# A two-layer relational graph convolution on one core: preparation at one part per quad, layer 2's weights after it, layer 2's table begun at quad 84

## The chip, the cores and the metric

The kernel runs on one core of a Trainium2 chip. The core has five engines that run side by side and wait for each other through semaphores: PE (matrix multiply), DVE (elementwise), ACT (activation and copies), POOL (here only the issue of gathers) and SP (here only the issue of plain transfers). The metric is the time of one execution on the device, in microseconds (us). Three runs of the kernel before took 4668.13, 4668.17 and 4673.87 us, a median of 4668.17. One more execution was profiled: it took 3997.74 us, and its profile spans 3996.0 us from the first to the last instruction. It is thus 670 us shorter than the runs that were only timed; the two are kept apart below.

## The reference

A graph has N = 12500 nodes with 128 features and E = 200000 edges, each with a source, a destination and one of R = 8 types; edges are sorted by destination. Two layers follow each other, then a residual and a normalization:

```python
W = einsum('rb,bio->rio', comp, basis)          # 8 weights of 128 x 128
msgs = einsum('ni,rio->nro', h, W)[src, et]     # one message per edge
seg = dst * 8 + et
mean = segment_sum(msgs, seg) / maximum(count(seg), 1)
h = h + relu(mean.reshape(N, 8, 128).sum(1) + h @ root + bias)   # twice
out = layernorm(x + h)
```

So each edge's message is divided by the number of edges with the same destination and type. All numbers are float32.

## The kernel before, in words

Edges are cut into 1563 tiles of 128. Four tiles are a quad (391 of them, `q`), eight a group (`g`, two quads), and 128 nodes a block (`k`, 98 of them; about four quads of edges end in one block).

**The gathers.** For every tile, in both layers, POOL issues one indirect transfer that fetches 128 rows of 128 numbers: rows of x in layer 1, rows of the table `y_d` in layer 2 (`gather`, L603). One `gather` call issues a quad. Rows land in a ring of 14 buffers, so the gather of quad q+14 waits until PE has used the rows of quad q; the loop asks for them 12 quads ahead. Three semaphores go round, so a quad's gather also waits for the landing of the one three before.

**Layer 1**, per quad: DVE makes one-hot matrices `dm` scaled by 1/count (`onehot`, L885, for two quads ahead); PE multiplies the gathered rows with them (`means`, L945) and ACT copies the result to `sT`. Per group, PE multiplies the eight types' means with the eight weights (`product`, L966), DVE makes a placement matrix (`place_in`, L977), and PE adds the group's rows to its block (`place`, L999, with the root product at L1001). When a block is full, `finish` adds bias and residual on ACT and DVE (L1015, L1032, L1033) and leaves the block of h in `hT`, in SBUF, where all 98 blocks stay. `table` then makes layer 2's messages of that block for every type: two halves, each one matmul (L1045) and one copy of 128 x 512, the second with the 512 KB store to `y_d` by SP.

**Layer 2** gathers rows of `y_d` with one edge each, sums them with one-hots (L1078), places and finishes as before, and `norms` writes the output. Its first gather waits for the whole of `y_d`. That gives a gap between the layers.

**Preparation.** One-hots and gathers need index tables, in four sets of blocks of 128 tiles. The first set is made before the loop. The others come from a generator, `prep`, inside layer 1's loop. For each set it yields 17 parts from `counts` (one that makes a key from destination and type; 12 that compare the key with itself shifted by four distances each, L726, and add the hits up with eight f16 matmuls, L732 and L733; and four that make `kr`, `w`, `idy` and `slot`, each with a transpose on PE, L689), and two parts more in all for the sources (`sources`, L703, L699). So there are 53 parts. The results of a compare part stand in a ring of two (`eq`).

**Weights.** `weight(l, r)` makes one 128 x 128 weight from eight bases: eight DVE instructions (L618, then L623 seven times). The eight of layer 1 are made before the loop, the eight of layer 2 in its first eight quads.

**Order.** Everything is written out by hand: the Python loop calls the steps in order, `Plan` appends each to the queue of its engine and works out the waits, and each engine runs its own queue strictly in that order. Small jobs hang in the list `todo`: loads and turns of x (`load_x`, `turn_x`), and the halves of the table. One is taken per quad, in three quads of four:

```python
if q % 4 != 3 and todo:
    todo.pop(0)()
if q < R:
    weight(1, q)
if parts is not None:
    if run(parts, 2):
        parts = None
elif later:
    later.pop()()
```

`later` holds the checks of the input's order (`check_edges` and others), one per quad after preparation.

**The arena.** `hT` shares its memory with what is only needed early (edge lists, bases, keys, the compare results). These lie from block `HA` on, so a block of h from there on is written only when what it covers has been read. `HA` is 8.

Of the kernel before, what the change touches and what calls it, by code (L numbers as in the profile page):

```python
# [415 lines left out]
def ordered_path(  # L416
# [30 lines left out]
    R = comp.shape[1]  # L447
# [4 lines left out]
    B = -(-T // P)  # L452
# [12 lines left out]
    S = 8  # L465
    GN = P * S
    NX = -(-N // GN)
    HA = 8
    assert D == P and R * K == P and B == BF + 1 and 1 < TL and LAST < P and BF % 4 == 0 and NQ % 2 == 1 and N % 2 == 0
    main = slice(HALO, HALO + P)  # L470

# [26 lines left out]
    over = {}  # L498
    at = HA * P

# [73 lines left out]
    def vec(emit, reads=(), writes=()):  # L574
        plan.add("DVE", emit, reads, writes)
# [4 lines left out]
    def pe(emit, reads=(), writes=()):  # L580
        plan.add("PE", emit, reads, writes)
# [4 lines left out]
    def load(out_t, in_t, reads=(), writes=(), q="SP"):  # L586
        e = nc.sync if q == "SP" else nc.scalar
        plan.add(q, lambda: e.dma_start(out_t, in_t), reads, writes, lane="hw" if q == "SP" else "aq")

    def copy(out_t, in_t, reads, writes):  # L590
        act(lambda: nc.scalar.activation(out_t, in_t, AF.Copy), reads, writes)  # L591
# [3 lines left out]
    def gather(l, q):  # L595
        if q >= NQ:
            return
        t, cell = rows_r.take()
        rows_g[l, q] = (t, cell)
        ids = idx if l == 0 else idy  # L600

        def emit():
            return [nc.gpsimd.indirect_dma_start(  # L603
                out=t[:, i - q * Q, :], out_offset=None, in_=x if l == 0 else y_d,
                in_offset=bass.IndirectOffsetOnAxis(ap=ids[:, i:i + 1], axis=0))
                for i in range(q * Q, min((q + 1) * Q, T))]

        b = q * Q // P
        reads = ["idx0" if l == 0 and q == 0 else ("idx", b)] if l == 0 else [("idy", b)]
        if l == 1 and q == 0:  # L610
            reads += [("y_d", j) for j in range(NT - 2)] + [("y_d", j, k) for j in (NT - 2, NT - 1) for k in (0, 1)]
        plan.add("POOL", emit, reads, [cell], lane="gq", n=min(Q, T - q * Q))

    def weight(l, r):
        c0 = (l * R + r) * NB

        def emit0():
            return nc.vector.tensor_scalar(w_sb[:, l, r, :], b_sb[:, l, 0, :], comp_sb[:, c0:c0 + 1], None,  # L618
                                           op0=ALU.mult)

        vec(emit0, [("b_sb", l), "comp"], [("w", l, r)])
        for b in range(1, NB):
            vec(lambda b=b: nc.vector.scalar_tensor_tensor(  # L623
                w_sb[:, l, r, :], b_sb[:, l, b, :], comp_sb[:, c0 + b:c0 + b + 1], w_sb[:, l, r, :],
                op0=ALU.mult, op1=ALU.add), [], [("w", l, r)])
# [171 lines left out]
    def check_edges(b):  # L797
        dxc = [("dx", b), ("dx", b, 1), ("dx", b, 2), ("dx", b, 3), ("pad", "dx")]
        t, tc_ = turns.take()
        v1, v2, v3 = (t[:, i, :] for i in range(3))  # L800
        c1, c2, c3 = tc_, tc_ + (1,), tc_ + (2,)
        for emit, r, wr in (
            (lambda: nc.vector.tensor_tensor(v1, dx[:, b, HALO + 1:HALO + P + 1], dx[:, b, main], op=ALU.is_lt),
             dxc, c1),
            (lambda: nc.vector.tensor_tensor(v2, dx[:, b, 2 * HALO:2 * HALO + P], dx[:, b, main], op=ALU.subtract),
             dxc, c2),
            (lambda: nc.vector.tensor_scalar(v3, v2, 250.0, None, op0=ALU.is_gt), [c2], c3),
            (lambda: nc.vector.tensor_tensor(v1, v1, v3, op=ALU.max), [c3], c1),
            (lambda: nc.vector.tensor_scalar(v3, v2, 1.0, None, op0=ALU.is_lt), [c2], c3),
            (lambda: nc.vector.tensor_tensor(v1, v1, v3, op=ALU.max), [c3], c1),  # L810
            (lambda: nc.vector.tensor_reduce(fails[:, b:b + 1], v1, axis=AX.X, op=ALU.max), [c1], ("fails", b)),
        ):
            vec(emit, r, [wr])
# [49 lines left out]
    def rows_of(j):  # L863
        return min(P, N - j * P)
# [11 lines left out]
    def onehot(l, q):  # L876
        if q >= NQ:
            return
        t, cell = dm_r.take()
        dms[l, q] = (t, cell)  # L880
        m, ids = (P, kr) if l == 0 else (2 * K, slot)

        def emit():
            for i in range(q * Q, q * Q + in_quad(q)):
                last = nc.vector.tensor_scalar(t[:, i - q * Q, :m], cols[:, :m], ids[:, i:i + 1],  # L885
                                               w[:, i:i + 1], op0=ALU.is_equal, op1=ALU.mult)
            return last

        b = q * Q // P
        vec(emit, ["cols", ("kr" if l == 0 else "slot", b), ("wt", b)], [cell])  # L890


    def shape_of(n):
        m = min(GN, N - n * GN)
        return (P, S) if m == GN else (m // 2, 2)
# [39 lines left out]
    def two_blocks(g):  # L935
        return (g + 1) // 2 - 1
# [37 lines left out]
    def place_in(g):  # L974
        m = tiles_of(g) * K
        t, c = pl[g] = pl_r.take()
        vec(lambda: nc.vector.tensor_scalar(t[:m], cols[:m], pos[:m, g // (2 * R), g % (2 * R):g % (2 * R) + 1],  # L977
                                            None, op0=ALU.is_equal), ["cols", "pos"], [c])
# [59 lines left out]
    def table(j):  # L1038
        n = rows_of(j)
        yr, yrc = yr_r.take()  # L1040
        split = j >= NT - 2

        def half(k):
            hb, bc = ct_b if split and k == 1 else pt_b
            pe(lambda: nc.tensor.matmul(hb[:n].rearrange("p r d -> p (r d)"), hT[:, j * P:j * P + n],  # L1045
                                        w_sb[:, 1, k * H:(k + 1) * H, :].rearrange("p r d -> p (r d)"),
                                        start=True, stop=True),
               [("h", j)] + [("w", 1, r) for r in range(k * H, (k + 1) * H)], [bc])
            if split and k == 1:
                vec(lambda: nc.vector.tensor_copy(yr[:n, H:, :], hb[:n]), [bc], [yrc + (k,)])  # L1050
            else:
                copy(yr[:n, k * H:(k + 1) * H, :], hb[:n], [bc], [yrc + (k,)])
            if split:
                load(y_d[j * P * R:(j * P + n) * R, :].rearrange("(p r) d -> p r d", r=R)[:, k * H:(k + 1) * H, :],
                     yr[:n, k * H:(k + 1) * H, :], [yrc + (k,)], [("y_d", j, k)])
            elif k == 1:
                load(y_d[j * P * R:(j * P + n) * R, :].rearrange("(p r) d -> p (r d)", r=R),
                     yr[:n].rearrange("p r d -> p (r d)"), [yrc + (0,), yrc + (1,)], [("y_d", j)])

        todo.extend([lambda: half(0), lambda: half(1)])  # L1060

    todo = []


    sum_b = [y_b, ct_b]
# [74 lines left out]
    def run(gen, n):  # L1140
        for _ in range(n):
            if next(gen, gen) is gen:
                return True
        return False
# [23 lines left out]
    def prep():  # L1168
        for i in range(1, len(groups)):
            if i + 1 < len(groups):  # L1170
                sources(*groups[i + 1])
                yield
            yield from counts(i)

    parts = prep()
    later = [lambda b=b: check_edges(b) for b in range(B)]
    later += [check_span, check_place, check_all]
    later.reverse()
    for q in range(NQ - 1):
        g = q * Q // G  # L1180
        gather(0, q + AHEAD)
        onehot(0, q + 2)
        if q == 1:
            where()
        if q % 2 == 0 and g > 0:
            place_in(g - 1)
        means(q)
        if q % 2 == 0:
            if g > 0:
                product(g - 1)  # L1190
        elif g > 0:
            place(0, g - 1)
            k, n = two_blocks(g - 1), two_blocks(g - 1) // S + 1
            if k % S == S // 2 and g % 2 == 1 and n < NX:
                todo.extend([lambda n=n, h=h: turn_x(n, h) for h in range(-(-shape_of(n)[1] // 4))])
                todo.append(lambda n=n: load_x(n + 1))
        if q % 4 != 3 and todo:
            todo.pop(0)()
        if q < R:
            weight(1, q)  # L1200
        if parts is not None:
            if run(parts, 2):
                parts = None
        elif later:
            later.pop()()
    g = NG - 1
    while todo:
        todo.pop(0)()
    place_in(g - 1)
    product(g - 1)  # L1210
    place_in(g)
    means(NQ - 1)
    place(0, g - 1)
    todo.pop(0)()
    product(g)
    todo.pop(0)()
    place(0, g)
    while todo:
        todo.pop(0)()

    for q in range(AHEAD):
        gather(1, q)
# [79 lines left out]
```

## Time and profile before

| | |
|---|---|
| median of three timed runs | 4668.17 us |
| profiled execution | 3997.74 us |
| its span | 3996.0 us |
| POOL busy | 2961.9 us, 74% |
| PE busy | 2093.2 us, 52% |
| DVE busy | 1378.5 us, 34% |
| ACT busy | 565.7 us, 14% |
| mean granted PE clock | 0.675 of full |
| last gather of layer 1, first of layer 2 begin | 2001.8 us, 2019.8 us |

The page gives busy time by engine, the chain of work that ended last, and groups of instructions. In a group's line stand the source line, engine, operation, output and inputs, count, busy time in us, the mean of one in ns, and the engine's idle time just before them with what ended most of it. "issue" is time in which the engine waited for nothing that the profile shows. Lines of a stage view give start and end, the length of the stage, the busy time and count of POOL's gathers in it, the granted PE clock, the busy share of the DMA engines and GB/s. Lines of waits give who waited, for whom, us in total, how often and the longest. Lines of a timeline give start, duration and instruction; its durations overlap where matmuls are pipelined.

### The profile page before, as it was taken

How to read it: one execution, taken by the hardware profiler on the slowest of the kernel's cores; microseconds unless marked ns; L12 is line 12 of the kernel's file. 1: busy time of each engine (PE TensorE's matmuls, PEld its weight loads, DVE VectorE, ACT ScalarE, POOL GpSimd, SP SyncE). 2: the span in 40 equal slices, each digit the busy share in tenths (PEclk: the TensorE clock that was granted, in tenths of full speed). 3: DMA queues.
4: the chain of work that ended last, by engine and by line, in shares of the span. 5: the costliest groups of instructions: out<-in, count | busy, mean ns of one | idle time of the engine just before them, and what ended most of it. 6: DMA issues, size and time to landing. Idle time of an engine off the chain costs nothing.

```text
span 3996.0 us, 33928 instructions
## 1 busy us (share of the span) xinstructions
PE 2093.2 (52%) x11597; PEld 1548.1 (39%) x11597; DVE 1378.5 (34%) x4770; ACT 565.7 (14%) x1238; POOL 2961.9 (74%) x3134
## 2 busy tenths in 40 slices
PE   4787666666666666676633333333333333333333
PEld 3466555555555555555522222222222222222221
DVE  8685333333333333333322332322323323223232
ACT  0123222222222222222200000000000000000000
POOL 7567777777777777777767777777777777777775
PEclk7899888888888878888865555555555555555555
DMA  3123222222222222222222222222222222222221
GB/s 108 52 78 95 79 85 79 85 85 85 79 85 79 85 79 85 85 81 79 79 69 53 64 64 53 63 53 64 63 53 64 63 53 63 53 63 63 53 59 48
DMA packets 128281, 282.59 MB, mean 71 GB/s; under 512 B 53327, under 2 KB 60763, under 8 KB 128099
## 3 DMA queue, kind: packets, MB, share of 16 engines
q0 software_dynamic: 100032, 205.07, 19.7%
q1 hardware_dynamic: 25546, 73.59, 4.9%
q8 instruction: 95, 1.56, 0.2%
q10 hardware_dynamic: 2521, 1.66, 0.2%
q14 instruction: 87, 0.71, 0.1%
HBM read 222.51 MB, written 57.60 MB: 70 GB/s over the span
## 4 chain that ended last, share of the span: by engine, by line
POOL 54%; issue 29%; DMA 7%; PE 4%; DVE 4%; ACT 0%; POOLq 0%; ACTq 0%; DVEq 0%; SPq 0%
POOL rows L603 54%; DMA rows<-in_x_dram,idx 5%; DMA rows<-y_d,idy 2%; PE s L945 1%; PE y L966 1%; DVE w_sb L623 1%; PE ct L732 1%; DVE dm L885 1%; PE ct L733 1%; DVE arena L726 1%; PE pt L1045 0%; PE pt L689 0%; DMA arena<-in_dst_dram 0%; PE po L999 0%; DVE arena L749 0%
## 5 line engine op out<-in xcount | busy, mean ns | idle before, releaser
L603 POOL DMA_INDIRECT rows<-in_x_dram,idx x1563 | 1485.9, 951 | 514.8 <-issue 440.8
L603 POOL DMA_INDIRECT rows<-y_d,idy x1563 | 1474.9, 944 | 493.1 <-issue 464.8
L945 PE MATMUL s<-dm,rows 128*128 128x128 f32 x3126 | 516.0, 317 | 535.6 <-DMA rows<-in_x_dram,idx 533.3
L945 PEld LDWEIGHTS s<-dm,rows 128*128 128x128 f32 x3126 | 454.2, 220 | 720.8 <-DMA rows<-in_x_dram,idx 554.3
L885 DVE TENSOR_SCALAR dm<-cols,kr,w 128x128 f32<-128x128 f32 x1563 | 530.8, 402 | 303.6 <-PE s L945 303.5
L1032 DVE TENSOR_TENSOR v<-po,carry 128x128 f32<-128x128 f32 x196 | 57.0, 291 | 1669.0 <-ACT carry L1015 1666.7
L885 DVE TENSOR_SCALAR dm<-cols,slot,w 128x32 f32<-128x32 f32 x1563 | 374.7, 302 | 501.9 <-PE y L1078 494.2
L1078 PE MATMUL y<-rows,dm 128*32 128x128 f32 x1568 | 210.7, 419 | 642.2 <-DMA rows<-y_d,idy 642.2
L1078 PE MATMUL ct<-rows,dm 128*32 128x128 f32 x1558 | 209.6, 419 | 592.5 <-DMA rows<-y_d,idy 592.5
L966 PE MATMUL y<-w_sb,sT 128*128 128x128 f32 x3136 | 512.0, 333 | 0.0
L966 PEld LDWEIGHTS y<-w_sb,sT 128*128 128x128 f32 x3136 | 500.5, 250 | 1.2 <-issue 1.0
L1078 PEld LDWEIGHTS y<-rows,dm 128*32 128x32 f32 x1568 | 119.2, 158 | 756.0 <-issue 396.7
L1078 PEld LDWEIGHTS ct<-rows,dm 128*32 128x32 f32 x1558 | 119.5, 158 | 666.6 <-issue 423.0
L999 PE MATMUL po<-pl,ys 128*128 128x256 f32 (+1 forms) x784 | 370.4, 567 | 12.2 <-DVE pl L977 9.5
L591 ACT ACTIVATE sT<-s 128x512 f32<-128x512 f32 x391 | 233.4, 597 | 963.8 <-PE s L945 963.5
L591 ACT ACTIVATE ys<-y 128x128 f32<-128x128 f32 (+1 forms) x294 | 81.4, 277 | 1118.5 <-PE y L1078 759.5
L1045 PE MATMUL pt<-w_sb,arena 128*128 128x512 f32 x388 | 208.1, 618 | 2.6 <-DVE arena L1033 2.6
L999 PEld LDWEIGHTS po<-pl,ys 128*128 128x128 f32 (+1 forms) x784 | 163.9, 261 | 89.5 <-issue 79.7
L977 DVE TENSOR_SCALAR pl<-cols,pos 128x256 f32<-128x256 f32 x392 | 186.0, 475 | 0.0
L591 ACT ACTIVATE ys<-ct 128x128 f32<-128x128 f32 x98 | 27.1, 277 | 939.4 <-PE ct L1078 939.4
L591 ACT ACTIVATE y_row<-pt 128x512 f32<-128x512 f32 x194 | 115.8, 597 | 162.1 <-PE pt L1045 162.1
L1015 ACT ACTIVATE carry<-po,bias_t 128x128 f32<-128x128 f32 x196 | 71.6, 365 | 97.3 <-PE po L999 97.3
(114 smaller groups left out, 910.1 us busy)
## 6 DMA issues: line engine op xcount, KB each, us to landing
y_d<-y_row SPq DMA_DIRECT2D x96, 512.0 KB, 2.9
rows<-in_x_dram,idx POOLq DMA_INDIRECT x1563
rows<-y_d,idy POOLq DMA_INDIRECT x1563
x_g<-in_x_dram SPq DMA_DIRECT2D x24, 512.0 KB, 3.7
out_dram<-x_g SPq DMA_DIRECT2D x12, 512.0 KB, 3.0
arena<-in_L_gnn_basis_dram SPq DMA_DIRECT2D x2, 512.0 KB
arena<-in_dst_dram ACTq DMA_DIRECT2D x2, 448.0 KB, 9.1
arena<-in_edge_type_dram SPq DMA_DIRECT2D x2, 448.0 KB, 13.2
```

Of the source, the lines that this page charges most:

```text
L591: act(lambda: nc.scalar.activation(out_t, in_t, AF.Copy), reads, writes)
L603: return [nc.gpsimd.indirect_dma_start(out=t[:, i - q * Q, :], out_offset=None, in_=x if l == 0 else y_d, in_offset=bass.IndirectOffsetOnA ...
L623: vec(lambda b=b: nc.vector.scalar_tensor_tensor(w_sb[:, l, r, :], b_sb[:, l, b, :], comp_sb[:, c0 + b:c0 + b + 1], w_sb[:, l, r, :], op0= ...
L885: last = nc.vector.tensor_scalar(t[:, i - q * Q, :m], cols[:, :m], ids[:, i:i + 1], w[:, i:i + 1], op0=ALU.is_equal, op1=ALU.mult)
L945: last = nc.tensor.matmul(s[:, i, :], t[:, i, :], d[:, i, :P], start=True, stop=True)
L966: last = nc.tensor.matmul(y[:m], t[:, r, :nt, :].rearrange("p t k -> p (t k)"), w_sb[:, 0, r, :], start=(r == 0), stop=(r == R - 1))
L977: vec(lambda: nc.vector.tensor_scalar(t[:m], cols[:m], pos[:m, g // (2 * R), g % (2 * R):g % (2 * R) + 1], None, op0=ALU.is_equal), ["cols ...
L999: ins = nc.tensor.matmul(a, o[:m], t[:m], start=opens, stop=last and not root_in)
L1015: act(lambda: nc.scalar.activation(nt, a[:, P:], AF.Identity, bias=bias_t[:, l:l + 1]), [ac, ("bias_t", l)], [ncell])
L1032: vec(lambda: nc.vector.tensor_add(v[:, :n], a[:, :n], t[:, :n]), [ac, c], [vc])
L1045: pe(lambda: nc.tensor.matmul(hb[:n].rearrange("p r d -> p (r d)"), hT[:, j * P:j * P + n], w_sb[:, 1, k * H:(k + 1) * H, :].rearrange("p ...
L1078: last = nc.tensor.matmul(y[j:j + 2 * K, :], d[:, i, :2 * K], t[:, i, :], start=(i % 2 == 0), stop=(i % 2 == 1 or i == n - 1))
```

## The change

Preparation takes one part per quad in place of two. The eight weights of layer 2 leave the first eight quads and become the first entries of `later`, so they come after preparation and ahead of the checks. The halves of the table go to a list of their own, `tables`, which is opened at quad 84: from there one half is taken in a quad where `todo` is empty and which isn't every fourth. Until then the blocks of h wait in `hT`. Jobs in `todo` may now be taken in every quad. The early data begin at block 24 of the arena in place of block 8. At the end of the loop what is left of both lists is issued, then the last group follows as before.

```diff
-    HA = 8
+    HA = 24
+    TABLE = 84
...
-        todo.extend([lambda: half(0), lambda: half(1)])
-
-    todo = []
+        tables.extend([lambda: half(0), lambda: half(1)])
+
+    todo, tables = [], []
...
-    later = [lambda b=b: check_edges(b) for b in range(B)]
+    later = [lambda r=r: weight(1, r) for r in range(R)] + [lambda b=b: check_edges(b) for b in range(B)]
...
-        if q % 4 != 3 and todo:
+        if todo:
             todo.pop(0)()
-        if q < R:
-            weight(1, q)
+        elif q % 4 != 3 and q >= TABLE and tables:
+            tables.pop(0)()
         if parts is not None:
-            if run(parts, 2):
+            if run(parts, 1):
                 parts = None
         elif later:
             later.pop()()
     g = NG - 1
-    while todo:
-        todo.pop(0)()
+    assert parts is None and not later
+    while todo or tables:
+        (todo or tables).pop(0)()
     place_in(g - 1)
     product(g - 1)
     place_in(g)
     means(NQ - 1)
     place(0, g - 1)
-    todo.pop(0)()
+    tables.pop(0)()
     product(g)
-    todo.pop(0)()
+    tables.pop(0)()
     place(0, g)
-    while todo:
-        todo.pop(0)()
+    while tables:
+        tables.pop(0)()
```

## The prediction

> **What bounds the kernel now.** I read the page first: busy shares, the chain that ended last, the costliest groups.
>
> ```profile
> PE 2093.2 (52%) x11597; PEld 1548.1 (39%) x11597; DVE 1378.5 (34%) x4770; ACT 565.7 (14%) x1238; POOL 2961.9 (74%) x3134
> POOL 54%; issue 29%; DMA 7%; PE 4%; DVE 4%; ACT 0%; POOLq 0%; ACTq 0%; DVEq 0%; SPq 0%
> L603 POOL DMA_INDIRECT rows<-in_x_dram,idx x1563 | 1485.9, 951 | 514.8 <-issue 440.8
> L603 POOL DMA_INDIRECT rows<-y_d,idy x1563 | 1474.9, 944 | 493.1 <-issue 464.8
> ```
>
> POOL's 3126 gathers are nearly the whole span: 0.944 us each and a fixed 0.30 us between two, 1.25 us per tile and 4.99 us per quad of four. 3126 x 1.25 is 3900 of 3996 us. A change can only save what POOL loses beyond that. Where it loses it is in the gathers by stages of 50 us, and in POOL's waits:
>
> ```profile
> 50.00:100.00 50.00, 38.56 (x38) 0.76 0.20 51
> 100.00:150.00 50.00, 26.90 (x27) 0.80 0.16 45
> 150.00:200.00 50.00, 29.22 (x29) 0.93 0.20 59
> 200.00:250.00 50.00, 31.17 (x31) 0.97 0.22 63
> 250.00:300.00 50.00, 37.65 (x40) 1.00 0.31 94
> ```
>
> ```profile
> POOL rows L603 <- issue: 905.6, 2971, 0.5
> POOL rows L603 <- PE s L945: 45.1, 26, 8.0
> POOL rows L603 <- DMA rows<-in_x_dram,idx: 22.6, 74, 0.3
> POOL rows L603 <- DMA y_d<-y_row: 17.1, 1, 17.1
> ```
>
> Steady state is 40 gathers in 50 us; from 100 to 250 us there are 27, 29 and 31. The wait is for PE's `means` (L945), 43.0 us of it before 270 us (the same view for that window), because a gather's buffer is free when `means` of 14 quads earlier is done. The 17.1 us is the gap between the layers.
>
> Why PE is late there, from PE's timeline at full clock:
>
> ```profile
> 211.21 1.05 PE L945 MATMUL s<-dm,rows 128*128 128x128 f32 x8
> 212.10 1.95 PE L966 MATMUL y<-w_sb,sT 128*128 128x128 f32 x16
> 213.89 1.02 PE L1045 MATMUL pt<-w_sb,arena 128*128 128x512 f32 x2
> 214.75 0.38 PE L732 MATMUL ct<-arena,id_h 128*128 128x512 f16 x1
> ...
> 218.22 1.05 PE L945 MATMUL s<-dm,rows 128*128 128x128 f32 x8
> 219.11 0.60 PE L999 MATMUL po<-pl,ys 128*128 128x256 f32 x2
> ```
>
> By start to start: means 0.89 us, product 1.79, half a table 0.86, place 0.43, and two counting parts, 16 f16 matmuls, 3.47 (1.73 a part). From one `means` to the next is 7.0 us where POOL needs 4.99. DVE adds to it: for the first eight quads a weight of layer 2 (one L618, seven L623: 2.9 us) stands in its queue beside the parts, and later an eq block (L726) waits for the `means` of its own quad (16.7 us of such waits from 60 to 260 us), for which PE then waits.
>
> **What the Trainium skill says.** "Perfetto Trace Analysis", DMA Instruction — SWDGE (GPSIMD): a gather's span ends when its descriptors are written, not when data lands. The trace agrees: `means` waits for rows after the gather's span. So POOL's 1.25 us is generation, which more DMA room doesn't shorten. "TensorE: Matmul & The Clock Gate", What's actually happening: PE runs at half clock after an idle window of about 3.4 us, at full clock after as long a busy one. The trace has both rates, 0.217 and 0.427 us per 512-column f16 matmul. "SBUF — State Buffer", Who interferes with whom: some DVE instructions hold a port that GpSimd needs. Here gathers beside f16 eq blocks take up to 1.27 us, once 2.73; to 270 us they average 1.006.
>
> **The change part by part.** *One part per quad.* Preparation is 53 parts: 36 eq parts, 12 with four transposes each, 2 `sources`, 3 that only make keys. It ended in quad 26 and will end in quad 53. The work is the same, so this saves POOL time only if PE's `means` keeps ahead of it. PE's work over these 53 quads at full clock:
> - 53 x (0.89 + half of 1.79 + half of 0.43 + a quarter of 0.22 for the root) = 53 x 2.05 = 109 us
> - 36 eq parts x 1.73 = 62 us
> - 14 transposing parts and four turns of x, 18 x 0.44 = 8 us
> - table halves: none now (0.86 each before).
>
> That is 179 us, and 201 at the clock 0.89 of the window 60 to 260 us. PE also waits for DVE. In every fourth quad DVE first finishes a block (L1032, L1033), then makes the eq block, and PE idles some 2.4 us (2.23 to 2.83 in the trace): 13 x 2.4 = 31. Three reciprocals (3.35 us and what goes with them) add 4 each, 12. The sum is 244 us, 4.6 per quad, against POOL's 4.99 and more. DVE's own quad is 1.36 (one-hots) + half of 0.47 + 0.15 + 1.9 (eq) = 3.6 us, so DVE isn't the bound.
>
> PE starts quad 1 at about 60 us. POOL unhindered starts the gather of quad q+14 at 3.4 + 4.99 (q+14) = 78 us for q = 1, so there are 18 us of slack besides. PE ends quad 53 at 60 + 244 = 304 us; POOL asks for it at 3.4 + 67 x 4.99 + 14 = 352. No stall is left: -43.0 us, and -0.6 for two short waits on place.
>
> *What comes back.* To 270 us gathers took 175 x (1.006 - 0.944) = 10.8 us above the usual, from overlap with eq blocks. POOL stood for a quarter of that stretch, so with no standing the same blocks meet more gathers: 10.8 / 0.77 - 10.8 = +3.2 us (between 0 and 6).
>
> *Layer 2's weights* (64 DVE instructions, 8 x 2.9 = 23 us) go from quads 0-7 to quads 54-61, where DVE has 5.0 - 1.8 us free per quad: nothing, hidden under POOL. Without that cover it would be 2.9 us per quad. First use is quad 84, so nobody waits. The checks follow to quad 77, 2 us each, hidden likewise.
>
> *The table.* 40 halves wait at quad 83. From 84, three quads in four take one while two come per four; by the order of issue the backlog is gone about quad 290. PE then has 2.05 + 0.65 = 2.7 us per quad, 5.4 at half clock; at its layer-1 clock of 0.83 it is 3.3, under 4.99. ACT's copy (0.60) and the 512 KB store move with each pair; stores come every 2.7 quads in place of 4, so DMA's share of 0.28 gains half of the stores' third, to about 0.33. SP has only these and loads of x. Nothing on POOL. The last halves before the gap (block 95, quads 388 and 389) and the flush stand as before, so the 17.1 us stay. Turns of x may now go in any quad: 0. A larger arena: 0, h above block 24 only meets regions read long before.
>
> *Sum:* -43.0 - 0.6 + 3.2 = -40.4 us. The profiled execution took 3997.7 us (1.7 around the span), so it would take 3957, 1.0% less. The runs' median is 670 us above it, and no view shows where. Spread over the gathers that is 0.21 us each. "Advanced Engine Details and Errata", Clock Domains, gives 1.18 to 1.25 times the usual cost at a lower power profile; 4668/3998 is 1.17. No run shows that this is the reason. If all is slower in proportion, the gain is 47 us (4621); if the excess lies elsewhere, it is 40 (4628). I take 4627.
>
> **Rivals.** *Only POOL is slower in unprofiled runs.* With 5.84 us per quad (4.99 + 0.86) much of the standing vanishes in the kernel before: quad 24's `means` is done at 239.7 us, POOL would ask for it at 3.4 + 38 x 5.84 = 225, so it lost only 14 us. The gain is then 14 - 3 = 11: 4657. For it: an excess this large fits 3126 gathers. Against: no trace of it.
>
> *The wait stays in part.* If the finishing quads and reciprocals cost PE twice what I took (86 us), or preparation runs at clock 0.75, PE needs about 5.4 to 5.5 us per quad; the slack then ends near the last quads and little is lost. With both it needs 6.2, and 60 + 52 x 6.2 - 352 = 30 us of waiting stays: 4655. Against it: the densest stretch before ran at 0.93 to 1.00.
>
> *Slower: PE falls to half clock in preparation.* One part leaves gaps where two filled PE. At clock 0.5, 179/0.5 + 43 = 401 us; PE ends quad 53 at 461 where POOL wants 352: 109 us standing in place of 43, so 4668 + 66 + 3 = 4737. It decides from about 6.4 us per quad, a mean clock of 0.62. Layer 2 runs at 0.50 with PE a third busy, which speaks for it; steady layer 1, with longer gaps than these (up to 3.4 us), holds 0.83, against.
>
> *No change.* If unprofiled layer 1 is bound by PE, its work is only shuffled: 4668 within a few us.
>
> **How the numbers follow.** Likeliest, 0.62: the standing goes, 4612 to 4636. POOL-only 0.18 (4650 to 4664), part 0.08 (4636 to 4660), no change 0.07, slower 0.05. A measurement tells about 0.2% (9 us) from no change; POOL-only is within that in a sixth of its chance, and the part case hardly ever. Faster 0.62 + 0.15 + 0.07 = 0.84, same 0.10, slower 0.06. The range goes from 4612 (gain in proportion, with no return) to 4664, and leaves out the no-change and slower cases.
>
> **What would show it.** In the profile after: POOL's wait on `means` before 400 us under 5 us, 40 gathers in each 50 us (38 beside eq blocks); PE waiting for rows in preparation; the gap between layers again about 17 us; table matmuls from some 430 us on, none before. It is wrong if POOL still waits for `means` between 100 and 350 us, if PE's clock there is under 0.65, or if the span falls 40 us and the unprofiled time doesn't.

## The result and the profile after

The kernel after takes 4641.05 us (median of four runs, 4639.45 to 4648.58), the kernel before 4668.15 beside it (four runs, 4667.5 to 4673.87). The ratio is 0.9942 with an interval of 0.9925 to 0.9960: 27 us or 0.58% faster. The forecast was 4627, the range 4612 to 4664.

After's profiled execution took 4641.36 us, as long as its timed runs. The profile of the kernel before that the prediction was made from, 3997.74 us, was an exception: the unchanged kernel, profiled again as the first experiment, took 4668.09 us, and no later profile was far from its own timed runs. So two comparisons must be kept apart. What the change did is read between after and that second profile of before (span 4666.3 us). What the first profile left out is read between the two profiles of before.

The page of after, in the lines that answer to those shown of before:

```profile
PE 1976.8 (43%) x11597; PEld 1485.4 (32%) x11597; DVE 1369.3 (30%) x4770; ACT 540.9 (12%) x1238; POOL 2971.1 (64%) x3134
another core or an unknown queue 53%; PE 22%; issue 12%; POOL 5%; ACT 4%; DVE 4%; DMA 0%; POOLq 0%; SPq 0%
L604 POOL DMA_INDIRECT rows<-in_x_dram,idx x1563 | 1495.3, 957 | 824.1 <-issue 434.6
L604 POOL DMA_INDIRECT rows<-y_d,idy x1563 | 1474.7, 944 | 799.4 <-issue 447.1
```

The gathers cost what they did (957 and 944 ns against 951 and 944), but POOL is busy for 64% of the span and not for 74%: the idle time before them grew from 1008 to 1624 us. The chain is no longer POOL's. Half of it goes to "another core or an unknown queue", which on this one core means a release that the profile has no record of; in the lists of waits it is called "remote". POOL's waits in after, us in total, how often, the longest:

```profile
POOL rows L604 <- issue: 881.7, 2872, 1.9
POOL rows L604 <- remote: 501.1, 161, 13.1
POOL rows L604 <- PE s L946: 140.2, 45, 25.2
POOL rows L604 <- DMA y_d<-y_row: 48.5, 1, 48.5
```

The same kernel before, in its second profile:

```profile
POOL rows L603 <- issue: 850.7, 2768, 1.2
POOL rows L603 <- remote: 503.7, 159, 12.5
POOL rows L603 <- PE s L945: 180.9, 72, 29.8
POOL rows L603 <- DMA y_d<-y_row: 44.5, 1, 44.5
```

So 504 us of unnamed waits and 181 us of waits for `means` belong to the usual execution of the kernel before, where the first profile had 45 for `means` and none unnamed. The change takes 41 us off the waits for `means` and leaves the unnamed ones. The waits before 260 us alone show the place; before first, after second:

```profile
POOL rows L603 <- PE s L945: 96.0, 17, 29.8
```

```profile
POOL rows L604 <- PE s L946: 57.5, 5, 25.2
POOL rows L604 <- remote: 8.0, 3, 2.7
```

96.0 us become 57.5 + 8.0: 30.5 us less. Outside preparation hardly anything changed; the gap between the layers is 4 us longer (48.5 for 44.5), and so it is with the pace alone (48.0). These are POOL's gathers by stages (start and end, length, busy and count, granted PE clock, DMA share, GB/s), the second profile of before:

```profile
100.00:200.00 100.00, 34.61 (x35) 0.93 0.08 23
200.00:300.00 100.00, 60.35 (x59) 0.93 0.19 59
600.00:1000.00 400.00, 260.67 (x276) 0.78 0.23 71
3000.00:3400.00 400.00, 267.37 (x283) 0.52 0.18 52
```

and after:

```profile
100.00:200.00 100.00, 54.79 (x51) 0.75 0.13 33
200.00:300.00 100.00, 65.17 (x65) 0.83 0.18 49
600.00:1000.00 400.00, 258.73 (x275) 0.80 0.26 77
3000.00:3400.00 400.00, 265.14 (x281) 0.53 0.19 52
```

From 100 to 300 us there are 22 gathers more. In steady layer 1, 275 stand against 276 in 400 us, 1.45 us per tile, and in layer 2 281 against 283, 1.42. The first profile had 321 and 322 in stretches of 400 us: 1.25.

**Where the 27 us are won, and some lost again.** ACT copies each quad's `means` to `sT`, so the starts of these copies tell when each quad was done (us; from the timelines):

| quad | 0 | 1 | 5 | 13 | 26 | 40 | 53 |
|---|---|---|---|---|---|---|---|
| before, first profile (3996.0) | 32.9 | 65.0 | 96.6 | 164.4 | 250.8 | 298.4 | 336.1 |
| before, second profile (4666.3) | 96.5 | 131.0 | 162.0 | 229.5 | 316.6 | 391.0 | 474.3 |
| after | 97.2 | 127.2 | 141.4 | 198.6 | 280.0 | 361.4 | 443.9 |
| lead of after over the second | -0.8 | 3.8 | 20.6 | 30.9 | 36.6 | 29.6 | 30.4 |

After leads by 36.6 us at quad 26, where before's preparation is over, and by 30.4 at quad 53, where its own is: 6.2 us are given back. The lead of a single quad swings by some 5 us either way (25.2 to 35.8 from quad 50 to 55, 29.7 in the mean). At the last quad of layer 1 it is 26.6 us, which is the timed gain.

**Why the usual execution is longer.** In both kernels quad 0 is done only at 97 us. DVE and PE make the tables of the first set, and each compare block (L727) needs a place whose counting matmuls are done. DVE's timeline in after (start, duration, instruction, idle time before it and who ended that):

```profile
38.22 0.69 DVE L727 TENSOR_TENSOR arena<-arena 128x153 f16<-128x153 f16 x4 [17.60 <-remote]
60.62 0.75 DVE L727 TENSOR_TENSOR arena<-arena 128x157 f16<-128x157 f16 x4 [21.71 <-remote]
79.53 0.70 DVE L727 TENSOR_TENSOR arena<-arena 128x161 f16<-128x161 f16 x4 [18.16 <-remote]
82.39 1.34 DVE L727 TENSOR_TENSOR arena<-arena 128x165 f16<-128x165 f16 x8 [2.15 <-PE ct L734]
```

PE ended the matmuls of the first of these blocks at 40.0 us and did nothing until 61.43; DVE's next block began at 60.62, 20.6 us after the last word that PE had to give. It needed even less: places go round in a ring of two, so its place was that of the block before those shown, whose matmuls had ended at 21.7 us, 38.9 us earlier. In the other direction nothing is late: PE begins at 38.97 us, 0.06 us after DVE's block is done. POOL issues gathers without a pause until 73.3 us and then stands. From 80 us on DVE goes on promptly. In the first profile the same blocks came one after the other although gathers were in flight:

```profile
10.15 0.68 DVE L726 TENSOR_TENSOR arena<-arena 128x149 f16<-128x149 f16 x4 [0.19 <-PE ct L733]
11.08 4.28 DVE L726 TENSOR_TENSOR arena<-arena 128x153 f16<-128x153 f16 x23 [0.26 <-PE ct L733]
```

The instructions are as long in both (0.68 us for the block of 149); what differs is the wait between them. From before's first profile to its second I estimate 578 us from the slower steady pace (1563 x (1.449 - 1.246) + 1563 x (1.413 - 1.246)), 53 from the waits for `means` at the start (96.0 for 43.0) and 27 from the gap between the layers (44.5 for 17.1): 658 of 670 us.

### The profile page after: what moved, and what is told of

Same layout as the page of the kernel before. It is cut to its first block, busy times and chain, and to the rows that moved or that the text cites. A ratio compares the mean times of both kernels' runs of the same rounds, so it can differ in the third digit from the quotient of the medians.

```text
span 4639.6 us, 33935 instructions
## 1 busy us (share of the span) xinstructions
PE 1976.8 (43%) x11597; PEld 1485.4 (32%) x11597; DVE 1369.3 (30%) x4770; ACT 540.9 (12%) x1238; POOL 2971.1 (64%) x3134
## 4 chain that ended last, share of the span: by engine, by line
another core or an unknown queue 53%; PE 22%; issue 12%; POOL 5%; ACT 4%; DVE 4%; DMA 0%; POOLq 0%; SPq 0%
PE s L946 7%; PE y L967 5%; POOL rows L604 5%; PE po L1000 3%; PE pt L1046 3%; ACT sT L592 2%; ACT ys L592 1%; DVE dm L886 1%; ACT carry L1016 1%; PE po L1002 1%; PE ct L733 1%; PE ct L1079 1%; PE ct L734 1%; PE s L1111 0%
## 5 line engine op out<-in xcount | busy, mean ns | idle before, releaser
L604 POOL DMA_INDIRECT rows<-in_x_dram,idx x1563 | 1495.3, 957 | 824.1 <-issue 434.6
L1000 PE MATMUL po<-pl,ys 128*128 128x256 f32 (+1 forms) x784 | 404.3, 612 | 1834.8 <-DVE pl L978 978.9
L946 PEld LDWEIGHTS s<-dm,rows 128*128 128x128 f32 x3126 | 492.1, 226 | 158.8 <-issue 138.6
L946 PE MATMUL s<-dm,rows 128*128 128x128 f32 x3126 | 500.7, 310 | 32.6 <-issue 29.7
L967 PE MATMUL y<-w_sb,sT 128*128 128x128 f32 x3136 | 459.0, 308 | 95.6 <-ACT sT L592 53.3
L967 PEld LDWEIGHTS y<-w_sb,sT 128*128 128x128 f32 x3136 | 439.3, 223 | 110.9 <-ACT sT L592 60.9
L1079 PE MATMUL y<-rows,dm 128*32 128x128 f32 x1568 | 157.4, 396 | 263.4 <-issue 142.1
L1046 PE MATMUL pt<-w_sb,arena 128*128 128x512 f32 x388 | 242.7, 712 | 46.6 <-issue 24.5
L1079 PEld LDWEIGHTS y<-rows,dm 128*32 128x32 f32 x1568 | 78.7, 149 | 345.4 <-issue 227.8
L1079 PE MATMUL ct<-rows,dm 128*32 128x128 f32 x1558 | 142.0, 416 | 85.2 <-issue 77.3
L733 PE MATMUL ct<-arena,id_h 128*128 128x512 f16 (+1 forms) x188 | 72.1, 404 | 110.9 <-DVE arena L727 60.6
L1079 PEld LDWEIGHTS ct<-rows,dm 128*32 128x32 f32 x1558 | 78.2, 157 | 111.6 <-issue 107.9
```

Of the source, the lines that this page charges most:

```text
L604: return [nc.gpsimd.indirect_dma_start(out=t[:, i - q * Q, :], out_offset=None, in_=x if l == 0 else y_d, in_offset=bass.IndirectOffsetOnA ...
L733: nc.tensor.matmul(ct[:, :nb, :], id_h, eq[:, s - s0, :nb, main], start=(s == 1), stop=False)
L946: last = nc.tensor.matmul(s[:, i, :], t[:, i, :], d[:, i, :P], start=True, stop=True)
L967: last = nc.tensor.matmul(y[:m], t[:, r, :nt, :].rearrange("p t k -> p (t k)"), w_sb[:, 0, r, :], start=(r == 0), stop=(r == R - 1))
L1000: ins = nc.tensor.matmul(a, o[:m], t[:m], start=opens, stop=last and not root_in)
L1079: last = nc.tensor.matmul(y[j:j + 2 * K, :], d[:, i, :2 * K], t[:, i, :], start=(i % 2 == 0), stop=(i % 2 == 1 or i == n - 1))
```

## The experiments

All times are medians, ratios against the kernel before timed beside them on the same chip. All kernels compute what the kernel before does. In the quoted expectations A and B are two views of the 670 us: results of other engines are heard late (A), or POOL itself is slower (B). A1 and A2 divide the change's gain between the pace of preparation and the jobs moved out of it; B1 puts the late first tables down to the gathers in flight; C1 and C2 are a pace of about 1.45 us per tile that nothing in the loop's buffers changes, and one set by the depth of the rings.

**The kernel before again, unchanged** (e0_same).

> The kernel before once more, unchanged, for a profile whose time is that of the timed runs. Theory A (the profile of 3996 us was an execution in which engines heard of each other's work at once; the timed runs are executions in which PE's results are announced late while gathers are in flight): time 4668 us, and this profile shows some 670 us of waits of POOL beyond the fixed 0.30 us, spread over both layers. Theory B (all instructions are slower by a sixth in the timed runs): gathers of 1.1 us in place of 0.944 and as few waits as in the profile before. Ratio 1.000 by both.

4670.71 us, ratio 1.0002 (0.9993 to 1.0010). Its gathers took 953 and 946 ns, so B falls. The time is in waits, as shown above: A.

**Only the pace** (e1_one_part): the kernel before with one line changed.

```diff
-            if run(parts, 2):
+            if run(parts, 1):
```

> One part of the change alone: preparation at one part per quad; layer 2's weights and the table where they were. Theory A1 (the gain is preparation's pace: POOL waits less for PE's means before quad 53): 0.4 to 0.6% faster, most of the 27 us of the whole change. Theory A2 (the gain comes from taking weights and table out of the first quads): 0 to 0.2% faster, under 10 us.

**Everything but the pace** (e2_two_parts): the kernel after with that line set back.

```diff
-            if run(parts, 1):
+            if run(parts, 2):
```

> The whole change but for the pace: preparation again at two parts per quad, weights after it (quads 27 to 34), table from quad 84. Theory A1: within 0.2% of before. Theory A2: 0.4 to 0.6% faster.

**Only the table** (e3_table_late): as e2_two_parts, with layer 2's weights in the first eight quads again. It is the kernel before with `HA`, `TABLE`, the list `tables` and the taking of jobs as after.

```diff
-    later = [lambda r=r: weight(1, r) for r in range(R)] + [lambda b=b: check_edges(b) for b in range(B)]
+    later = [lambda b=b: check_edges(b) for b in range(B)]
...
+        if q < R:
+            weight(1, q)
...
-            if run(parts, 1):
+            if run(parts, 2):
```

> Only the table is moved (its own list, from quad 84) and the small jobs may go in any quad; weights in the first eight quads, preparation at two parts per quad. Theory A1: within 0.2% of before. Theory A2: some of the gain, 0.1 to 0.5%, and the rest of it is the weights' when compared with the kernel of two parts.

| | time (before beside it: 4669.8) | ratio | POOL's wait for `means` to 260 us | lead at quad 26 and 53 |
|---|---|---|---|---|
| before again | 4670.71 | 1.0002 (0.9993 to 1.0010) | 96.0 | 0 and 0 |
| table alone | 4664.56, -5.2 | 0.9987 (0.9980 to 0.9994) | 94.1 | 5.5 and 11.2 |
| table and weights | 4655.64, -14.2 | 0.9961 (0.9947 to 0.9975) | 81.2 | 15.9 and 20.7 |
| pace alone | 4654.61, -15.2 | 0.9965 (0.9954 to 0.9976) | 64.1 | 30.5 and 16.6 |
| after | 4641.05 (own comparison: -27.1) | 0.9942 (0.9925 to 0.9960) | 57.5 | 36.6 and 30.4 |

Neither division holds: the pace is worth some 15 us, the weights some 9, the table some 5, and they add up (29.4) to about the whole (27.1). The intervals of the table alone and of table with weights don't meet, so the weights' share is real; so is the table's, which lies just outside no change. The pace takes away by far the most waiting and then gives nearly half back: its lead falls from 30.5 to 16.6 us between quads 26 and 53 (17.1 in the mean of quads 50 to 55). The two moves keep theirs (6.1 and 15.2 in that mean).

**Gathers wait for the first tables** (x1_gathers_wait): the gathers of quads 1 to 11 are issued after the first set, and wait for its last table.

```diff
+        if l == 0 and q > 0:
+            reads.append(("slot", 0))
...
-    for q in range(AHEAD):
-        gather(0, q)
+    gather(0, 0)
...
+    for q in range(1, AHEAD):
+        gather(0, q)
```

> The kernel after, but all gathers except the first quad's wait for the end of the first set of index tables, so that almost no gather is in flight while that set is made. Theory B1 (PE's results are announced some 20 us late while gathers are in flight, promptly otherwise): the first set takes 20 us in place of 85, means of quad 0 comes near 35 us in place of 97, and the 15 us that POOL starts later are more than won back: 4600 to 4625 us. Theory B2 (the lateness doesn't depend on the gathers): 15 us slower than the kernel after, 4650 to 4660 us.

4622.84 us, ratio 0.9895 (0.9879 to 0.9912). POOL stands for 15.9 us more at the start, and yet the kernel is 18 us faster than after. DVE's timeline, at the same blocks:

```profile
7.54 0.66 DVE L729 TENSOR_TENSOR arena<-arena 128x137 f16<-128x137 f16 x4 [0.57 <-PE ct L736]
8.39 0.66 DVE L729 TENSOR_TENSOR arena<-arena 128x141 f16<-128x141 f16 x4 [0.20 <-issue]
9.32 5.41 DVE L729 TENSOR_TENSOR arena<-arena 128x145 f16<-128x145 f16 x31 [0.27 <-PE ct L736]
```

With only one quad of gathers issued, DVE hears PE within 0.2 to 0.6 us. Quad 0's copy to `sT` comes at 31.38 us in place of 97.22. B1 holds: what differs from after is when the gathers are issued. Once they flow again, from 24.27 us on, things are late again, and quad 1 is copied only at 98.15 us. It isn't PE's results alone that are late then. Each of the seven later steps of a weight waits for nothing but the step before it, on DVE itself; at 40 us seven take 2.68 us, and some 20 us later DVE idles for 1.05 us before most of them:

```profile
40.36 2.68 DVE L626 SCALAR_TENSOR_TENSOR w_sb<-arena,comp_sb,w_sb 128x128 f32<-128x128 f32 x7
61.05 0.35 DVE L626 SCALAR_TENSOR_TENSOR w_sb<-arena,comp_sb,w_sb 128x128 f32<-128x128 f32 x1 [1.05 <-DVE w_sb L626]
62.45 0.35 DVE L626 SCALAR_TENSOR_TENSOR w_sb<-arena,comp_sb,w_sb 128x128 f32<-128x128 f32 x1 [1.05 <-DVE w_sb L626]
```

**Room for the first compare results** (x2_eight_slots): the first set's compare results get eight places, so DVE seldom needs PE's word.

```diff
+            also = []
+            if b0 == 0:
+                u = s0 // S4 // 2 % 4
+                eq, also, ec = eq[:, :, u:u + 1], [ec + (s - s0,) for s in ss], ec + ("first", u)
...
-            pe(emit, [ec + (s - s0,) for s in ss] + ["id_h"], [cc])
+            pe(emit, [ec + (s - s0,) for s in ss] + also + ["id_h"], [cc])
```

> The kernel after, but the compare results of the first set have eight places in place of two (each needs a quarter of a place), so DVE makes eight of the twelve without waiting for PE. If DVE's waits for PE's late announcements are what delays the first quads, the first set ends some 40 to 60 us earlier, and the time falls by 15 to 45 us to 4595 to 4625 us. If POOL's early waits come from elsewhere, within 5 us of the kernel after.

4620.02 us, ratio 0.9898 (0.9882 to 0.9915). Quad 0 is copied at 47.74 us, and POOL's waits for `means` before 260 us are these:

```profile
POOL rows L604 <- PE s L950: 24.7, 4, 18.0
POOL rows L604 <- remote: 8.8, 4, 2.5
```

33 us of the 57.5 are gone, 21 in the time, as expected. It supports B1 from the other side: the gathers run as before, only the number of times that DVE must hear PE is smaller.

**A pause of POOL in every quad** (x3_pause_quad) and **in every tile** (x4_pause_tile). POOL fills an unused buffer and drains after one gather of each quad, or after each gather (with 128 columns).

```diff
+                if i % 4 == 0:
+                    nc.gpsimd.iota(idle, pattern=[[1, 256]], base=0, channel_multiplier=0)
+                    nc.gpsimd.drain()
```

> The kernel after with a small iota and a drain on POOL after the first gather of every quad, so gathers come a little less densely, about 1.35 us per tile. Theory B1 in its strong form (announcements are late because landings come faster than they can be taken): PE's results are announced sooner, POOL waits less, and the time falls below the kernel after although POOL does more, to 4300 to 4600 us. Theory B2: POOL's extra work disappears in its waits, 4635 to 4660 us. If POOL were simply the bound in the timed runs: 4641 + 390 x 2 x 0.4, about 4950 us.

> The kernel after with an iota of 128x128 and a drain after every gather, about 1.5 to 1.6 us per tile. Theory B1: announcements are prompt, POOL waits only for itself, and the time is 3126 times POOL's own step, 4700 to 5000 us, with a mean PE wait of POOL near none. Theory B2: the waits stay and add to it, over 5000 us, or stay hidden, 4641.

5681.97 us (ratio 1.2167, 1.2146 to 1.2187) and 10298.86 us (2.2048, 2.2011 to 2.2085). POOL's timeline with a pause per quad:

```profile
1000.28 0.36 POOL L611 IOTA idle<- 128x256 int32 x1
1002.70 0.95 POOL L607 DMA_INDIRECT rows<-in_x_dram,idx  x1 [2.06 <-issue]
1003.95 0.95 POOL L607 DMA_INDIRECT rows<-in_x_dram,idx  x1 [0.30 <-issue]
```

The pause adds 2.1 us to a quad, 4 x 1.25 + 2.1 = 7.1; 391 x 2 quads of 7.1 us are 5552 of the span of 5680.9. With a pause in every tile a tile takes 3.3 us; both drains cost more than was expected, and both times lie far outside what either theory gave. As a remedy they fail; what they test are the waits. These are POOL's waits with a pause per quad:

```profile
POOL rows L607 <- issue: 2361.0, 3092, 8.4
POOL rows L607 <- DMA y_d<-y_row: 19.5, 1, 19.5
```

No wait for `means`, none unnamed: POOL's own work sets the pace. Quad 0 is copied at 30.71 us and quad 1 at 60.73, and the gap between the layers is 19.5 us: three figures near before's first profile (32.9, 65.0, 17.1) and far from its second (96.5, 131.0, 44.5). What is late becomes prompt with a pause in each quad. A pause holds both a gap in the gathers and a drain of POOL; which of the two does it isn't separated.

**Three compare buffers** (x5_eq_three): x2_eight_slots with a ring of three, so twelve places for the first set, and `HA` at 16 to make room.

```diff
-    HA = 24
+    HA = 16
...
-    eq_f = [early(S4 * 4 * C // 2, F16, f"eq{i}", [("eq", i, s) for s in range(S4)]) for i in range(2)]
+    eq_f = [early(S4 * 4 * C // 2, F16, f"eq{i}", [("eq", i, s) for s in range(S4)]) for i in range(3)]
...
+                u = s0 // S4 // 3 % 4
```

> The kernel with eight places for the first set, and now a ring of three compare results in place of two (twelve places for the first set; early data from block 16 of the arena). If DVE's waits for PE's late announcements in the compare blocks also cost time inside the loop, 5 to 15 us under the kernel with eight places (4605 to 4615); if not, the same 4620 within 5 us.

4615.11 us, ratio 0.9883 (0.9867 to 0.9900), the lowest median of all, 55 us under the kernel before. It is 4.9 us under x2_eight_slots, and the intervals of the two overlap, so the question isn't decided: this is neither clearly the 5 to 15 us that waits inside the loop would give nor clearly none. Its lead over before is 62.0 us at quad 53 and 56.1 at the end of layer 1.

**Deeper rings in the loop.** Eight one-hot buffers in place of four (x6_dm_eight), or gathers asked for 16 quads ahead with 18 buffers (x7_ahead_16), both with `HA` at 16.

```diff
-    dm_r = Ring(const, 4, [P, Q, P], F32, "dm")
+    dm_r = Ring(const, 8, [P, Q, P], F32, "dm")
```

```diff
-    AHEAD = 12
+    AHEAD = 16
```

> The kernel after with eight one-hot buffers in place of four (early data from block 16), so DVE doesn't wait for PE's announcement of two quads ago but of six. Theory C1 (the steady 1.45 us per tile is a rate at which announcements and landings can be taken): steady pace unchanged, 4630 to 4645 us. Theory C2 (the steady pace is the chain of engines that wait for each other's late announcements): faster in both layers, under 4550 us.

> The kernel after with gathers 16 quads ahead in place of 12 and 18 buffers in place of 14 (early data from block 16). C1: steady pace unchanged; POOL may run 16 tiles further before its first wait, which helps preparation by at most the 20 us of four quads: 4615 to 4645 us. C2: longer lateness is covered, steady pace better, under 4550 us.

4635.03 us (0.9923, 0.9906 to 0.9939), not to be told from after, and 4657.20 us (0.9971, 0.9962 to 0.9979), about 14 us slower than after by the ratios. In steady layer 1 both have 276 gathers in 400 us, as before, so the depth of these two rings doesn't set it, and C2 falls as far as they test it. Why the second is slower was a miss, and its timeline answers it: quad 0 is copied at 118.69 us, 21.5 us after that of after. Four more buffers are 4 x 4.99 = 20 us more of gathers before POOL first stands, and only then do the first tables get on. That fits the same lateness, made worse by a deeper ring.

**A pause in every fourth quad** (x8_pause_16): as x3_pause_quad with `if i % 16 == 0`; POOL's own step is then (16 x 1.25 + 2.1) / 16 = 1.38 us per tile.

> The kernel after with the iota and drain once in four quads, which cost 2.1 us each time: POOL's own step is 1.25 + 0.13 = 1.38 us per tile. C1 with a rate of 1.45 us per tile: the pauses only take the place of POOL's waits, 4635 to 4660 us. If pauses let the announcements through and then nothing else binds: 3126 x 1.38 and some 60 us of start and gap, about 4380 us. C2: in between.

4715.30 us, ratio 1.0091 (1.0075 to 1.0108), some 55 us over what was expected. POOL's waits:

```profile
POOL rows L607 <- remote: 138.6, 65, 3.8
POOL rows L607 <- PE s L952: 21.8, 17, 2.8
```

The unnamed waits fall from 501 to 139 us and those for `means` from 140 to 22, but the 196 pauses (about 410 us) take their place. In steady layer 1 there are 266 gathers in 400 us, 1.50 us per tile. DVE's longest unnamed wait before a one-hot falls from 48.2 to 15.2 us. So rare pauses make the announcements less late without bringing the 1.25 back; they exchange one loss for another. C1's fixed pace of 1.45 isn't confirmed either, since pauses that only took the place of waits would have left it.

## Why the prediction was right, and where it was not

**Right: the place, the direction, and the rest untouched.** The gain lies in preparation, in POOL's wait for `means`; no other stage became faster. The range held the time. But the likeliest case's own range, 4612 to 4636, did not: 4641 lies in that of the rival "the wait stays in part". That the total came near has luck in it: the prediction drew its whole gain from the pace, which is worth some 15 us, and the other half came from the weights and the table, which it had put at nothing.

**Wrong: "PE starts quad 1 at about 60 us ... 18 us of slack besides ... No stall is left".** This is the step that failed. In usual executions quad 1 is done only near 127 us (131 in the second profile of before), since the first set's tables wait for late words of PE. There is no slack but a debt: in after POOL stands 24.2 us for quad 0 and 25.2 for quad 1, and the pace hardly touches these (alone it leads by 1.0 us at quad 1). The term of -43.0 is -96.0 + 57.5 + 8.0 = -30.5 us in the profiles.

**Wrong: "4.6 per quad".** From quad 1 to quad 53 after's copies are (443.9 - 127.2) / 52 = 6.09 us apart. The rival had named 6.2 as the pace at which waiting stays, and part of its reasons came true: the granted clock was 0.75 and 0.83 from 100 to 300 us, where the kernel before has 0.93 in both. At 0.79 the 179 us of PE's work are 227, and with the 43 us of waits for DVE 5.1 us per quad (an estimate). The rest wasn't taken apart; it lies in the stretch where results are heard late. 0.62, from which the slower rival decides, wasn't reached.

**Not foreseen: a longer preparation costs.** Between quads 26 and 53 after needs 6.07 us per quad, while before, done with its preparation, needs 5.84. That is 6.2 us given back; 13.9 with the pace alone. "What comes back" had named a different thing, gathers stretched by compare blocks, at +3.2 us. The Trainium skill's "SBUF — State Buffer", Who interferes with whom, says that a DVE instruction with two inputs in SBUF, as a compare block is, contends with a GpSimd instruction that reads SBUF. The trace of after agrees: gathers that begin with a compare block, at 132.16 and 137.94 us, take 2.37 and 2.44 us in place of 0.94. But the layer-1 gathers are busy 6.5 us longer in after (1495.3 for 1488.8) and no longer with the pace alone (1488.6), where most is given back. So stretched gathers don't explain it, and what does stays open.

**Wrong: "layer 2's weights: nothing, hidden under POOL".** They are worth 9 us. The cover was missing where they stood, not where they went: from quad 0 to 7 POOL stands and the chain of DVE and PE sets the time, and 23 us of weights stood in DVE's queue; that they delay this chain is my reading. It fits that the lead arises there: at quad 7 the kernel with table and weights moved leads by 10.3 us, the one with the table alone by none (-0.5). The wait for `means` is 12.9 us shorter without them there. The prediction had seen them in DVE's queue beside the parts, but put them at nothing, because it believed that the pace alone ended all waiting.

**The table: half right.** In steady layer 1 it costs POOL nothing (275 and 276 gathers) and lifts the DMA share from 0.23 to 0.26, as forecast in direction. Against "nothing", moving it is worth 5 us of the time (e3_table_late). Its first matmul came at 617 us, not at 430, by the slower start and pace. The gap between the layers is 48.5 us (44.5 before), not 17.1.

**The excess of 670 us: asked about, but not found.** It is neither in proportion nor in POOL's instructions. The Trainium skill's "Advanced Engine Details and Errata", Clock Domains, from which the prediction took a factor of 1.18 to 1.25 at a lower power profile, does not explain it: single instructions are as long in both profiles. It is waits, spread over both layers. That also undoes the rival "only POOL is slower": its size for the gain, 11 us, was for a POOL that asks late, while POOL here asks early and is answered late.

**Signs.** Of those that the prediction set, POOL's wait for `means` under 5 us and 40 gathers per 50 us did not come; its own test "wrong if POOL still waits for `means` between 100 and 350 us" came true as to the steps, though not as to the time. PE's `means` waited for rows for 1.0 us in all between 130 and 420 us.

**Open.** What delays the words isn't known. Shown is that it depends on when and how gathers are issued (x1_gathers_wait, x3_pause_quad). Why one execution of the kernel before heard everything promptly at full density is not known either. That the engines lack instructions is unlikely: in the stop in layer 2 shown below no packet of an instruction queue moved from 3008 to 3031 us, and all three engines went on. The trace of that prompt execution holds 56,279 semaphore updates, those with a pause in every quad or tile 50,974 and 56,458, and all others 14,278 to 16,051. So missing records and lateness come together, and "remote" names a gap in the record and no place. Whether one makes the other, or recording itself plays a part, no run tests.

## What to carry to other kernels

Before a sum is made from a profile, the profile's own time must stand beside the timed runs: where they are 17% apart, slack read from it (here 18 us) may not exist, and a second profile is worth more than any refinement of the sum. Where one engine issues gathers without a break, count how often other engines must hear each other before the first result, and give that stretch its own places or start the gathers after it; both were worth 18 to 26 us here on top of the change, nearly as much as the change itself. Work that is spread thinner over a loop isn't free while the loop's other chain is the slower one: look for the lead at the end of the stretch (26.6 us here), not for its largest value (36.6).

## What the runs showed of the hardware

While gathers were in flight at full density, DVE heard PE at least 16 to 21 us after its matmuls in the first set (24 to 40 us after those of the block whose place it needed), and within 0.2 to 0.6 us where only one quad had been issued (x1_gathers_wait). PE heard DVE within 0.1 us in the same stretch. In layer 2 after's timeline of DVE has a stop of the same length, which POOL and ACT end within the same 0.3 us (3030.71 and 3030.56 us):

```profile
3008.14 0.48 DVE L978 TENSOR_SCALAR pl<-cols,pos 128x256 f32<-128x256 f32 x1
3030.47 0.69 DVE L1117 TENSOR_TENSOR x_g<-s,x_g 128x512 f32<-128x512 f32 x1 [21.85 <-remote]
```

POOL's last gather before it had ended at 3026.16 us, some 4 us earlier; in the first set DVE went on at 79.53 us, 6 us after POOL's last gather. But DVE had gone on at 38.22 and 60.62 us too, while gathers ran.

The usual executions run at 1.42 to 1.45 us per tile where the first profile had 1.25. That the steady loss has the same cause as the late first set is an inference from the pauses, which removed POOL's unnamed waits wholly (one pause in each quad) or for the most part (one in four). A fill of 128 x 256 and a drain on POOL between gathers cost 2.1 us; in every tile the drain left 2.0 us idle each time, and yet the gathers kept their 0.95 us.
